# Quadrant moves of transposed attention probabilities: 16 SBUF-to-SBUF DMAs per block against one DMA to DRAM and four back

## The chip, the cores and the metric

The kernel runs on one core of a Trainium2 chip. The metric is the device time in microseconds (us) of one execution; three runs of the kernel before were timed, and one execution was recorded by the hardware profiler. Inside the core, TensorE (PE) multiplies matrices, VectorE (DVE), ScalarE (ACT) and GpSimd (POOL) do the elementwise work, and SyncE (SP) issues nearly all DMAs. Each engine works through its own instructions in order; semaphores hold an instruction back until what it reads is there.

## The reference

Two layers over a batch of 128 blocks of 128 x 512 fp32 numbers. Layer 0 mixes rows with `adj`, layer 1 is an attention with 8 heads of 64 over the 128 rows of each block, masked by `adj`.

```python
# layer 0: both weights are adj, so C - A is the bias b alone
A = einsum('od,bdn->bon', adj, x)
x1 = layernorm(x + max_n(relu(A + b)))       # the maximum is over the 512 columns
# layer 1
q, k, v = split(x1 @ w_qkv)                  # 8 heads of 64
p = softmax(where(adj == 0, -inf, q k^T / 8))
o = (p v) @ w_proj + b_proj
z = o + layernorm(o) * ln_gamma + ln_beta
out = layernorm(x1 + z)
```

## The kernel before

One block is one batch element: its 128 rows lie on the 128 SBUF partitions. Four blocks make a group (`G` = 4). The loop over steps `s` runs every stage once per step, for different blocks: in step `s` the scores of block `s`, the attention product and the projection of block `s-1`, the inner tail of block `s-2`, the output of block `s-3`, the layer 0 of block `s+11` and its normalization and transpose one step later, as block `s+10`; and two of the eight q/k products of the next group and one v product. So a step holds one block's share of every stage, and the blocks in flight are spread over about fourteen steps. At the end of the batch the q/k/v work stops first (no next group), then layer 0 has long stopped, and the last steps hold attention and tails alone.

What sets the order. The order of the matmuls is written out by hand: `pin` (`keep_in_program_order`) makes TensorE issue them as the program has them, which is, per step: scores (L214), a q/k unit (L174), layer 0 (L135), a q/k unit, the attention product of the block before (`attend`, L267), a v unit (L190), the projection (`project`, L284). The order on the other engines and on SP's DMA queue is chosen by the framework's scheduler when the kernel is built, from the dependences and the program order. Tiles come from pools with a given number of buffers (`bufs`, 2 if nothing else is said); whoever writes into a buffer again waits for its last reader.

Two transposes need help from DMA. VectorE's stream transpose works within 32 x 32 squares, so after it each square is transposed, but still in the quadrant of 32 partitions where it was. `move_quadrants` (L121 to L125) then moves 4 x 4 pieces between quadrants, with one DMA each, all issued by SP. It is used at two places:

- `prob_transpose` (L251 to L260), once per block. `softmax_div` has divided the exponentials, VectorE transposes the 128 x 1024 probabilities into `pu` (L255), and 16 DMAs of 32 partitions x 1 KB each bring them to `pT`. `attend` (L262 to L275) of the next step multiplies by `pT` on TensorE (L267, 16 small matmuls), and ACT copies the result to `oT` for the projection. `pu` and `pT` have two buffers each.
- `layer0_transpose` (L152 to L164), for every fourth block: the four blocks of a group are transposed into one tile `xt`, and after the fourth one 16 DMAs of 64 KB bring them to `x1T`, which the q/k and v products of the next group read three steps later.

SP's queue holds besides these the load of one `x` block per step (L79, from HBM) and the store of one result `res` per step (L310, to HBM).

Of the kernel before, what the change touches and what calls it, by code (L numbers as in the profile page):

```python
# [9 lines left out]
F32 = mybir.dt.float32  # L10
# [6 lines left out]
def kernel(  # L17
# [22 lines left out]

    nc = tc.nc
    B, P, D = x.shape
    H = 8
# [5 lines left out]
    Q = 4  # L51
    QS = P // Q
# [4 lines left out]
    const = ctx.enter_context(tc.tile_pool(name="const", bufs=1))  # L57
    sb = ctx.enter_context(tc.tile_pool(name="sb", bufs=2))
    small = ctx.enter_context(tc.tile_pool(name="small", bufs=4))
    ps_s = ctx.enter_context(tc.tile_pool(name="ps_s", bufs=3, space=bass.MemoryType.PSUM))  # L60
    ps_m = ctx.enter_context(tc.tile_pool(name="ps_m", bufs=4, space=bass.MemoryType.PSUM))
    ps_o = ctx.enter_context(tc.tile_pool(name="ps_o", bufs=1, space=bass.MemoryType.PSUM))
# [58 lines left out]
    def move_quadrants(dst, src):  # L121

        for i in range(Q):
            for q in range(Q):
                nc.sync.dma_start(out=dst[i][ds(q * QS, QS)], in_=src[q][ds(i * QS, QS)])  # L125
# [125 lines left out]
    def prob_transpose(b):  # L251

        p = prob.pop(b)
        u = sb.tile([P, Q, H, QS], F32, tag="pu", name=f"pu_{b}")
        nc.vector.transpose(  # L255
            u.rearrange("p q h b -> p h q b"), p.rearrange("p h (q a) -> p h q a", q=Q)
        )
        t = sb.tile([P, Q, H, QS], F32, tag="pT", name=f"pT_{b}")
        move_quadrants([t[:, i] for i in range(Q)], [u[:, q] for q in range(Q)])
        pT[b] = t  # L260

    def attend(b):  # L262
# [53 lines left out]
    for s in range(-(LA + 1), B + 4):  # L316
        g, j = divmod(s, G)
        nxt = g + 1
        has_next = 0 <= nxt < B // G
        if s > -(LA + 1):  # L320
            on(load, s + LA + 3)
        on(scores, s)
        on(tail_outer, s - 3)
        on(layer0_norm, s + LA)
        on(layer0_transpose, s + LA)
        if has_next:
            qk_unit(nxt, 2 * j)
        on(layer0, s + LA + 1)
        if has_next:
            qk_unit(nxt, 2 * j + 1)  # L330
        on(tail_inner, s - 2)
        on(attend, s - 1)
        if has_next:
            v_unit(s + G)
        on(layer0_stats, s + LA + 1)
        on(project, s - 1)
        on(softmax_div, s)
        on(prob_transpose, s)
        on(tail_residual, s - 2)
# [41 lines left out]
```

## Time and profile before

| | |
|---|---|
| device time, median of 3 runs | 2524.27 us (2522.86 to 2524.66) |
| profiled execution: its own time / its span | 2525.88 us / 2524.1 us |
| TensorE's granted clock, mean over the span | 0.948 |
| VectorE busy | 1532.6 us (61%), 2690 instructions |
| ScalarE busy | 700.1 us (28%) |
| GpSimd busy | 787.9 us (31%) |
| DMA | 407480 packets, 174.80 MB; queue of SP 27.6% of 16 engines |
| HBM read / written | 38.60 MB / 33.55 MB |
| longest wait: ACT for VectorE's row maximum (L236 for L233) | 1093.2 us in 128 times |

The device time of the profiled execution is its span, from the first to the last instruction, and 1.8 us around it. An engine's share of busy time says how much of the span it has work in hand; a wait of an engine matters only where that engine, or what waits for it in turn, sets the end. ACT's 1093.2 us is such a harmless wait: ACT has 28% of work and waits because it has nothing else to do.

### The profile page before, as it was taken

To read this page: it belongs to the slowest core of one execution; us is meant where nothing else is said; L and a number is where in the kernel's file an instruction comes from. 1 tells how busy PE (TensorE), PEld (TensorE's weight loads), DVE (VectorE), ACT (ScalarE), POOL (GpSimd) and SP (SyncE) were. 2 spreads that over 40 slices of the span, in tenths; PEclk is the share of its full clock that TensorE was granted. 3 is DMA by queue.
4 is the path that set the end of the run, shared out by engine and by line. 5 is a ranking of instruction groups with operands and counts; after the bars stand their busy time and mean duration, and the time that the engine had idled before them with its cause. 6 is when DMAs were issued, how large, how long until landed. Compare 5 with 4: busy or idle time off the path is not lost. (4 is left out here: it accounts for less than half of the span.)

```text
span 2524.1 us, 28394 instructions
## 1 busy us (share of the span) xinstructions
PE 2278.5 (90%) x8449; PEld 1087.7 (43%) x8449; DVE 1532.6 (61%) x2690; ACT 700.1 (28%) x2561; POOL 787.9 (31%) x1159
## 2 busy tenths in 40 slices
PE   5999999999999999999999999999999999998974
PEld 2444444444444444444444444444444444444432
DVE  4465666656666656656656666666656666655554
ACT  1222223232223232222232232322232322232221
POOL 1123333332333333333333333333333323332323
PEclk8999999999999999999999999999999999999986
DMA  5222332322332322332222233322332322322111
GB/s 165 48 62 68 71 76 66 72 68 68 71 77 65 72 68 69 71 74 67 71 67 70 71 75 69 71 69 68 71 72 68 72 70 66 70 62 60 41 47 42
DMA packets 407480, 174.80 MB, mean 69 GB/s; under 512 B 307488, under 2 KB 373152, under 8 KB 407328
## 3 DMA queue, kind: packets, MB, share of 16 engines
q1 hardware_dynamic: 405792, 168.02, 27.6%
q10 hardware_dynamic: 1536, 4.98, 0.5%
q8 instruction: 68, 1.11, 0.2%
q14 instruction: 84, 0.69, 0.1%
HBM read 38.60 MB, written 33.55 MB: 29 GB/s over the span
## 5 line engine op out<-in xcount | busy, mean ns | idle before, releaser
L174 PE MATMUL pq<-x1T,wqkv 128*128 128x512 f32 x2048 | 934.0, 600 | 16.3 <-DMA x1T<-xt 16.3
L236 ACT ACTIVATE s<-s,nmax 128x128 f32<-128x128 f32 x1024 | 396.1, 388 | 1093.2 <-DVE nmax L233 1093.2
L174 PEld LDWEIGHTS pq<-x1T,wqkv 128*128 128x128 f32 x2048 | 380.3, 190 | 462.9 <-issue 447.9
L190 PE MATMUL pv<-wqkv,x1T 128*128 128x512 f32 x1024 | 509.5, 643 | 0.0
L284 PE MATMUL pp<-wproj,oT 128*128 128x512 f32 x1024 | 473.5, 607 | 3.6 <-ACT oT L275 3.6
L267 PE MATMUL po<-pT,v 128*64 128x128 f32 x2048 | 168.7, 315 | 197.6 <-DMA pT<-pu 188.9
L304 DVE TENSOR_TENSOR z<-z,x 128x512 f32<-128x512 f32 x128 | 88.6, 692 | 420.5 <-POOL z L299 420.5
L284 PEld LDWEIGHTS pp<-wproj,oT 128*128 128x128 f32 x1024 | 199.4, 195 | 255.4 <-issue 249.7
L190 PEld LDWEIGHTS pv<-wqkv,x1T 128*128 128x128 f32 x1024 | 199.9, 206 | 232.7 <-issue 229.5
L114 POOL TENSOR_SCALAR rs_o<-mv_o 128x1 f32<-128x1 f32 x128 | 28.4, 222 | 769.8 <-DVE mv_o L112 769.8
L288 DVE TENSOR_TENSOR o<-pp,bp_bc 128x512 f32<-128x512 f32 x128 | 88.5, 692 | 295.8 <-PE pp L284 295.8
L267 PEld LDWEIGHTS po<-pT,v 128*64 128x64 f32 x2048 | 134.5, 158 | 295.2 <-issue 270.1
L297 POOL TENSOR_TENSOR z<-z,ga_bc 128x512 f32<-128x512 f32 x128 | 162.2, 1267 | 281.1 <-DVE z L119 281.1
L114 POOL TENSOR_SCALAR rs_y<-mv_y 128x1 f32<-128x1 f32 x128 | 28.3, 221 | 627.3 <-DVE mv_y L112 623.3
L198 ACT COPY v<-pv 128x512 f32<-128x512 f32 x128 | 74.9, 585 | 428.4 <-PE pv L190 428.4
L236 ACT ACTIVATION_READ_ACCUMULATOR s<-s,nmax 128x1 f32 x1024 | 191.4, 187 | 0.0
L223 DVE SCALAR_TENSOR_TENSOR s<-pss,mask 128x512 f32<-128x512 f32 x256 | 168.2, 658 | 2.9 <-PE pss L214 2.9
L214 PEld LDWEIGHTS pss<-qkT 64*128 64x128 f32 x2048 | 124.3, 188 | 97.2 <-issue 97.2
L299 POOL TENSOR_TENSOR z<-z,o 128x512 f32<-128x512 f32 x128 | 162.7, 1271 | 10.0
L298 POOL TENSOR_TENSOR z<-z,be_bc 128x512 f32<-128x512 f32 x128 | 162.3, 1268 | 10.0
L249 DVE TENSOR_TENSOR s<-s,rec 128x1024 f32<-128x1024 f32 x128 | 156.8, 1225 | 4.4
L255 DVE STREAM_TRANSPOSE pu<-s 128x1024 f32<-128x1024 f32 x128 | 157.1, 1227 | 0.1
(37 smaller groups left out, 1829.3 us busy)
## 6 DMA issues: line engine op xcount, KB each, us to landing
pT<-pu SPq DMA_DIRECT2D x2048, 32.0 KB, 1.8
x<-in_x_dram SPq DMA_DIRECT2D x128, 256.0 KB, 2.8
x1T<-xt SPq DMA_DIRECT2D x512, 64.0 KB, 2.3
out_dram<-res SPq DMA_DIRECT2D x128, 256.0 KB, 2.2
wqkv<-in_L_gnn_w_qkv_dram ACTq DMA_DIRECT2D x4, 768.0 KB, 7.5
wproj<-in_L_gnn_w_proj_dram ACTq DMA_DIRECT2D x1, 1024.0 KB, 9.2
bp_bc<-in_L_gnn_b_proj_dram ACTq DMA_DIRECT2D x1, 256.0 KB, 8.0
ga_bc<-in_L_gnn_ln_gamma_dram ACTq DMA_DIRECT2D x1, 256.0 KB, 8.3
```

The source lines that it names most:

```text
L174: pin(nc.tensor.matmul(pq, lhsT=wqkv[:, c, ts(m, P)], rhs=x1T[g][:, c, :], start=(c == 0), stop=(c == KC - 1),))
L190: pin(nc.tensor.matmul(pv, lhsT=x1T[g][:, c, ts(j, P)], rhs=wqkv[:, c, ds(2 * D, D)], start=(c == 0), stop=(c == KC - 1),))
L214: pin(nc.tensor.matmul(pss[par][:, pr, :], lhsT=qkT[g][rows, pr, ts(j, P)], rhs=qkT[g][rows, KC + pr, ts(j, P)], start=True, stop=True,))
L223: nc.vector.scalar_tensor_tensor(s[:, par], pss[par], SCALE, mask.unsqueeze(1).to_broadcast([P, NP, P]), ALU.mult, ALU.add,)
L236: nc.scalar.activation(p[:, i, :], p[:, i, :], AF.Exp, bias=nmax[:, i : i + 1], accum_out=sums[:, i : i + 1],)
L249: nc.vector.tensor_tensor(p, p, rec.unsqueeze(2).to_broadcast([P, H, P]), ALU.mult)
L255: nc.vector.transpose(u.rearrange("p q h b -> p h q b"), p.rearrange("p h (q a) -> p h q a", q=Q))
L267: pin(nc.tensor.matmul(po[ds(par * HD, HD), pr, :], lhsT=v[:, ds((2 * pr + par) * HD, HD)], rhs=t[:, :, par * NP + pr, :], start=True, sto ...
L284: pin(nc.tensor.matmul(pp, lhsT=o[:, c, :], rhs=wproj[:, c, :], start=(c == 0), stop=(c == KC - 1)))
L297: nc.gpsimd.tensor_tensor(z, z, ga_bc, ALU.mult)
L298: nc.gpsimd.tensor_tensor(z, z, be_bc, ALU.add)
L299: nc.gpsimd.tensor_tensor(z, z, o, ALU.add)
```

## The change

The helper stays as it is for `layer0_transpose`. `prob_transpose` no longer calls it. It takes a scratch tile `hop` in DRAM (three buffers), writes the whole of `pu` there with one DMA (128 partitions x 4 KB, 512 KB), and then reads it back with four DMAs, one for each quadrant of `pT`: each fills 32 partitions with four pieces of 1 KB per partition (128 KB). All five are issued by SP. The numbers in `pT` and their place are those of before. The reads take what the write has put into `hop`, so they depend on it.

```diff
@@ pools
     small = ctx.enter_context(tc.tile_pool(name="small", bufs=4))
+    dram = ctx.enter_context(tc.tile_pool(name="dram", bufs=3, space=bass.MemoryType.DRAM))
@@ prob_transpose
         nc.vector.transpose(
             u.rearrange("p q h b -> p h q b"), p.rearrange("p h (q a) -> p h q a", q=Q)
         )
+        hop = dram.tile([Q, QS, Q, H * QS], F32, tag="hop", name=f"hop_{b}")
+        nc.sync.dma_start(
+            out=hop.rearrange("i a q f -> (i a) (q f)"), in_=u.rearrange("p q h b -> p (q h b)")
+        )
         t = sb.tile([P, Q, H, QS], F32, tag="pT", name=f"pT_{b}")
-        move_quadrants([t[:, i] for i in range(Q)], [u[:, q] for q in range(Q)])
+        for q in range(Q):
+            nc.sync.dma_start(
+                out=t[ds(q * QS, QS)].rearrange("a i h b -> a i (h b)"),
+                in_=hop[:, :, q].rearrange("i a f -> a i f"),
+            )
         pT[b] = t
```

## The prediction

> **What bounds the kernel now.** I read the page's busy shares first, then the table of waits, then the timelines of TensorE and of SP around one stall, then the landing times of the DMAs.
>
> ```profile
> PE 2278.5 (90%) x8449; PEld 1087.7 (43%) x8449; DVE 1532.6 (61%) x2690; ACT 700.1 (28%) x2561; POOL 787.9 (31%) x1159
> ...
> PE po L267 <- DMA pT<-pu: 188.9, 43, 8.6
> PE pq L174 <- DMA x1T<-xt: 16.3, 1, 16.3
> ```
>
> TensorE has work for 90% of the span, and nearly all that it waits for is one thing: in 43 of 128 blocks the attention product waits for `pT`, 188.9 us in all. TensorE's timeline over five steps shows where (start, duration, line, operation; in brackets the idle time before and its releaser):
>
> ```profile
> 1247.15 1.09 PE L267 MATMUL po<-pT,v 128*64 128x128 f32 x16
> 1248.18 3.70 PE L190 MATMUL pv<-wqkv,x1T 128*128 128x512 f32 x8
> ...
> 1260.73 3.60 PE L174 MATMUL pq<-x1T,wqkv 128*128 128x512 f32 x8
> 1269.60 1.98 PE L267 MATMUL po<-pT,v 128*64 128x128 f32 x16 [5.27 <-DMA pT<-pu]
> 1271.50 4.42 PE L190 MATMUL pv<-wqkv,x1T 128*128 128x512 f32 x8
> ...
> 1288.30 1.09 PE L267 MATMUL po<-pT,v 128*64 128x128 f32 x16
> ...
> 1305.47 1.09 PE L267 MATMUL po<-pT,v 128*64 128x128 f32 x16
> ```
>
> One `attend` to the next is 17.1 us where nothing stalls (1230.05 to 1247.15), then 22.45, 18.70, 17.17 us. The stall of 5.27 us comes once per four steps, and it costs more than itself: after it the 16 matmuls take 1.98 instead of 1.09 us, and the v unit 4.42 instead of 3.70; TensorE runs at half clock for a moment. SP's timeline of the same stretch shows the cause:
>
> ```profile
> 1235.64 10.02 SPq L125 DMA_DIRECT2D pT<-pu  x16
> 1245.75 0.63 SPq L125 DMA_DIRECT2D x1T<-xt  x1
> 1246.48 0.56 SPq L310 DMA_DIRECT2D out_dram<-res  x1
> 1247.10 10.67 SPq L125 DMA_DIRECT2D x1T<-xt  x15
> 1257.89 10.26 SPq L125 DMA_DIRECT2D pT<-pu  x16
> ```
>
> Sixteen issues of `pT` keep SP busy for 10.0 us. In every fourth step sixteen issues of `x1T` (0.63 + 10.67 us) stand in front of the next `pT`: its `pu` is ready at 1252.80 (VectorE's transpose starts at 1251.57 and takes 1.23), but SP gets to it at 1257.89. The last piece lands at about 1269.5, and TensorE could have started at 1264.3. So the bound is TensorE, plus one stall per group that SP's issuing makes. Without `x1T` ahead it just fits: `pu` ready 1235.61, `attend` 1247.15.
>
> ```profile
> pT<-pu SPq DMA_DIRECT2D x2048, 32.0 KB, 1.8
> x<-in_x_dram SPq DMA_DIRECT2D x128, 256.0 KB, 2.8
> x1T<-xt SPq DMA_DIRECT2D x512, 64.0 KB, 2.3
> out_dram<-res SPq DMA_DIRECT2D x128, 256.0 KB, 2.2
> ```
>
> The last number is the median from issue to landing. It hardly grows with size: eight times the bytes of a `pT` piece add 0.4 us to HBM and 1.0 us from HBM.
>
> **What the Trainium skill says.** "Perfetto Trace Analysis", section What "DMA-bound" means: a kernel can be bound on the issuing engine's sequencer, whose track is then solid DMA slices, and fewer, larger transfers help. The trace agrees: 1235.64 to 1268.15 on SP is one row of issues. "DMA: Bandwidth & Descriptors", section Anatomy of one DMA: about 2 us of every DMA is fixed, most of it the confirmation that the last byte landed, and HBM is the heaviest target. The medians of 1.8 to 2.8 us agree in size; a store to HBM (2.2) is no worse than an `x1T` piece inside SBUF (2.3). Same page, section Two DMAs through the same engine are not ordered: a DMA that reads what another wrote must be issued only after the first one's semaphore, so the reads wait on SP for the write to land; no run so far shows such a wait. "TensorE: Matmul & The Clock Gate", section What's actually happening: after an idle window of about 3.4 us the array falls to half clock and needs about as long to recover. The trace agrees: gaps up to 1.14 us are followed by 1.09 us for the 16 matmuls, the gap of 5.27 us by 1.98.
>
> **The change part by part.** I call T the time from the end of the transpose into `pu` until the last part of `pT` has landed, SP being free. Now it is 0.1 us to the first issue, fifteen issue intervals of 10.02/16 = 0.63 (9.4), and 1.8 for the last to land: 11.3 us.
>
> *Removed:* sixteen issues per block, 10.0 us of SP, and their sixteen landings.
>
> *Added, the write.* Its issue costs 0.33 to 0.56 us (what L310's stores take). Landing: the store of 256 KB takes 2.2; twice the bytes are eight more packets of 2 KB per DMA engine, at 84 ns each (median of the packet records), 0.7: 2.9 us. Bounds: 2.2 (no more than half the bytes) and 4.1 (the slowest store, 3.4, plus 0.7).
>
> *Added, the wait.* SP stands still for these 2.9 us. Behind it on SP are the four reads, the next `x` load (two steps ahead of its use), `x1T` (three steps ahead) and the store (nobody waits for it but its buffer), so only the reads matter.
>
> *Added, four reads.* Issue 0.63 each as now (0.71 at most, the interval of `x1T`, which has more and smaller pieces): 1.9 from first to last. Landing: the 256 KB load takes 2.8, these have 128 KB in pieces of 1 KB, a little less: 2.6. Bounds: 1.8 (a `pT` piece today) and 4.3 (the slowest landing of any L125 DMA).
>
> T = 0.1 + 2.9 + 0.1 + 1.9 + 2.6 = 7.6 us; from the bounds, 6.1 to 10.7 (last with 2.1 for the issues). SP is held for about 5.5 us per block instead of 10.0, wait included. Buffers do not tighten: `pu` is free when the write has landed, earlier than now, `hop` has three, and the read into `pT` needs an `attend` one step earlier to be over, as now. The bytes through the DMA engines rise by 128 x 512 KB, 67 MB to 174.8; their share of 27.6% leaves room.
>
> *Moved: the collision.* With SP free at about 1241 instead of 1245.66, `x1T` starts earlier; its first issue may even fall into the wait (`xt` is ready at 1237.96). If the store stays between the first and the second issue, it waits for `res` (1242.74) and is done at 1243.3; fifteen issues of 0.71 end at 1254.0; the write follows, and `pT` is there at 1254.0 + 7.5 = 1261.5. TensorE wants it at 1264.25. The stall is gone with 2.7 us to spare. Without `x1T`, `pT` is there 7.6 us after `pu`, 3.9 us before TensorE asks. Next in line is then TensorE itself, at 17.1 us per step.
>
> *The sum*, against the profiled execution. From the first `attend` (109.6) to the 117th (2305.6) are 116 steps in 2196.0 us; 116 x 17.12 (17.10, and a little for the 17.17 to 17.2 that some smooth steps show) = 1986: 210 us less. The next six steps, to 2415.34, take 109.7; their TensorE work is 16.25 us each (2365.25 to 2381.49), 97.5: 12 less. In the last five steps TensorE waits for the loop attend, projection, scores, softmax, transpose, T, attend, which carries two steps: 33.94 us now (2433.20 to 2467.14), and it shrinks by 11.7 - 7.6 = 4.1; 2.5 times: 10 less. The start, up to the first `attend`, and the 23 us after the last one stay. 2525.88 - 232 = 2294 for this execution, and as the median of the runs lies 1.6 lower, 2292.
>
> **The rivals.**
>
> *A, slower hop, smaller gain.* From `attend` of one block to the `pu` two blocks later is 1252.8 - 1230.05 = 22.7 us, so two steps cannot be shorter than 22.7 + T. That is 34.2, TensorE's own pace, at T = 11.5, and the collided step is late from T = 10.2 on. A gap below some 3.4 us costs itself, a larger one 1.6 more. With T = 12.5, the collided step is 2.3 late and all others lose 0.5: 29 x 2.3 + 116 x 0.5 = 125 us back, about 2417. For it: a write and a read of the same scratch in HBM within microseconds is in no row of the trace. Against: no store or load of HBM in the steady part is near what it needs.
>
> *B, the hop eats all.* A step costs 2196/116 = 18.93 us now, so the break-even is 2 x 18.93 - 22.7 = 15.2 us for T. If write and read both landed like the 768 KB weights at the start (7.5 us), T = 17.1, two steps 39.8, a step 19.9: +112 over the 116 steps, some +25 behind them, 2660. Against: those weights were loaded all at once, together with the first blocks.
>
> *C, the reads are queued behind `x1T`; slower.* The scheduler sees that the reads are not ready when the write is issued, and may place SP's other work between. If all sixteen `x1T` issues and the store stand there, the reads start at 1254.0, `pT` lands at 1258.6, and `attend`, wanted at 1247.15, is 11.4 late plus 1.6 for the clock: 13.0 per group against the present 75.7 - 68.4 = 7.3. 29 groups x 5.7 = 165 slower, less the 22 won at the end: some 2670. It decides from seven such issues on (3.9 us of slack hold five or six at 0.71), and costs more than now from about twelve. For it: the store already stands between `x1T` issues today. Against: the reads belong to the earlier step and would be ready some 1 us after `xt` is.
>
> That the change moves different data is excluded by its indices; that TensorE stands at a lower clock when it no longer pauses is possible, but a stretch of 85 us (55 to 140) is on record at full clock.
>
> **How the numbers follow.** Forecast 0.63, within 2275 to 2320 (T anywhere from 6.1 to 10.7). A 0.18, reaching from 2320 to 2490. B 0.08, of which 0.04 ends near no change. C 0.11. Faster: 0.63 + 0.18 = 0.81. Within 0.2% (5 us, about what a measurement of this kernel can tell from no change): 0.04. Slower: 0.04 + 0.11 = 0.15. B and C are left out of the range, 0.19; it reaches from 2275 to 2450, over most of A.
>
> **What would show it.** Right: no wait of L267 for `pT` in the steady part, steps of 17.1 us throughout, the clock at full between 140 and 2250, SP waiting some 3 us per block for the write, T near 7.6 us. The write's landing shows the first term, the reads' the last. Wrong: stalls at every step (A or B), or SP's timeline with `x1T` between the write and the reads (C).

## The result, and the profile after

The changed kernel takes 2697.49 us (median; 2695.24 to 2698.57) against 2524.47 us for the kernel before on the same chip: a ratio of 1.0684, 95% interval 1.0665 to 1.0702. It is slower by 173 us, where 232 us less were forecast, and outside the stated range. The span of the profiled execution is 2696.2 us against 2524.1.

The lines of the page and of the table of waits that answer to those shown of the kernel before (the change moves the line numbers; `attend` is now L277):

```profile
PE 2265.9 (84%) x8449; PEld 1081.7 (40%) x8449; DVE 1532.5 (57%) x2690; ACT 699.6 (26%) x2561; POOL 789.7 (29%) x1159
...
PE po L277 <- DMA pT<-hop: 374.4, 35, 12.2
```

TensorE's and VectorE's busy times hardly changed. The wait for `pT` has become rarer, 35 times instead of 43, and twice as long in sum, 374.4 us instead of 188.9: the time went exactly where the prediction hoped to take it from. TensorE's timeline over five steps (start, duration, line, operation, idle time before):

```profile
1241.03 1.09 PE L277 MATMUL po<-pT,v 128*64 128x128 f32 x16
...
1258.13 1.09 PE L277 MATMUL po<-pT,v 128*64 128x128 f32 x16
...
1286.59 1.98 PE L277 MATMUL po<-pT,v 128*64 128x128 f32 x16 [11.28 <-DMA pT<-hop]
```

A step takes 17.10 us where nothing is late, and the next one 28.46. The pattern is once per group as before, but the stall is 11.28 us instead of 5.27. SP's timeline over the same steps:

```profile
1229.62 0.33 SPq L261 DMA_DIRECT2D hop<-pu  x1
1232.24 1.75 SPq L266 DMA_DIRECT2D pT<-hop  x4
...
1246.72 0.32 SPq L261 DMA_DIRECT2D hop<-pu  x1
1249.07 1.27 SPq L127 DMA_DIRECT2D x1T<-xt  x2
1250.44 1.99 SPq L266 DMA_DIRECT2D pT<-hop  x4
1253.74 0.36 SPq L320 DMA_DIRECT2D out_dram<-res  x1
1254.14 9.36 SPq L127 DMA_DIRECT2D x1T<-xt  x14
1263.82 0.34 SPq L261 DMA_DIRECT2D hop<-pu  x1
1270.85 0.34 SPq L320 DMA_DIRECT2D out_dram<-res  x1
1280.91 0.32 SPq L261 DMA_DIRECT2D hop<-pu  x1
1281.34 4.31 SPq L266 DMA_DIRECT2D pT<-hop  x8
```

The first write is followed by its four reads, as the diff has them. The write at 1263.82, the one behind `x1T`, is not. Behind it stand a store, then the write of the *next* block, and only then the reads of both blocks, eight of them. The next write waits for the next `pu`, whose transpose ends at 1280.9 (VectorE starts it at 1279.66 and takes 1.23). So the data of this block lie in DRAM from about 1266.4 on, nobody fetches them for 15 us, and TensorE stands.

The hop itself is fast. The page's landing times:

```profile
hop<-pu SPq DMA_DIRECT2D x128, 512.0 KB, 2.6
pT<-hop SPq DMA_DIRECT2D x512, 128.0 KB, 3.4
```

In the step at 1229.62 the last read is issued at 1233.6 and lands some 3.2 us later, about 7.2 us after `pu` was ready. The forecast for this T was 7.6.

The balance, from the starts of `attend` in the profiled execution: the 116 steps that took 2196.0 us now take 2376.6 (+181), the six after them 112.0 instead of 109.7 (+2), the last five 76.0 instead of 85.6 (-10). A group of four steps is 28.9 + 18.8 + 17.1 + 17.1 = 81.9 us, against 75.7 before and 68.4 without any stall; 30 steps of the whole execution are of the long kind.

### The profile page after: what moved, and what is told of

Read it like the earlier page. It is cut to its first block, busy times and chain, and to the rows that moved or that the text cites. A ratio compares the mean times of both kernels' runs of the same rounds, so it can differ in the third digit from the quotient of the medians.

```text
span 2696.2 us, 26511 instructions
## 1 busy us (share of the span) xinstructions
PE 2265.9 (84%) x8449; PEld 1081.7 (40%) x8449; DVE 1532.5 (57%) x2690; ACT 699.6 (26%) x2561; POOL 789.7 (29%) x1159
## 4 chain that ended last, share of the span: by engine, by line
PE 73%; DVE 10%; POOL 7%; DMA 5%; SPq 3%; issue 2%; ACT 0%; POOLq 0%; ACTq 0%
PE pq L176 26%; PE pv L192 18%; PE pp L294 17%; PE po L277 6%; DMA pT<-hop 4%; PE pss L216 4%; PE pa L137 3%; SPq L266 2%; POOL z L308 2%; POOL z L307 2%; POOL z L309 2%; DVE nmax L235 1%; DVE pu L257 1%; DVE o L298 1%; DVE st_o L112 1%
## 5 line engine op out<-in xcount | busy, mean ns | idle before, releaser
L192 PE MATMUL pv<-wqkv,x1T 128*128 128x512 f32 x1024 | 500.1, 633 | 0.0
L277 PE MATMUL po<-pT,v 128*64 128x128 f32 x2048 | 168.8, 316 | 374.4 <-DMA pT<-hop 374.4
L277 PEld LDWEIGHTS po<-pT,v 128*64 128x64 f32 x2048 | 133.7, 159 | 470.4 <-issue 470.4
L285 ACT COPY oT<-po 128x512 f32<-128x512 f32 x128 | 74.9, 585 | 409.2 <-PE po L277 400.0
```

The source lines that it names most:

```text
L192: pin(nc.tensor.matmul(pv, lhsT=x1T[g][:, c, ts(j, P)], rhs=wqkv[:, c, ds(2 * D, D)], start=(c == 0), stop=(c == KC - 1),))
L277: pin(nc.tensor.matmul(po[ds(par * HD, HD), pr, :], lhsT=v[:, ds((2 * pr + par) * HD, HD)], rhs=t[:, :, par * NP + pr, :], start=True, sto ...
```

## The experiments

Three theories were put against each other. O: the loss is the place of the reads on SP's queue, and nothing else. H: a hop through HBM is too slow for the steps with `x1T`. S: the sixteen `x1T` issues clog SP, whatever comes behind them.

### Reads held directly behind their own write

Only edges of issue order on SP's queue are added, no wait for completion. They keep whatever SP is given later (loads, `x1T`, writes into `hop`, stores, each wrapped as the load is here) behind the last read, so that all 128 writes are followed at once by their four reads:

```diff
+    last_read = []
+    def behind_reads():
+        return tc.issue_after(last_read[0].ins) if last_read else nullcontext()
...
-        nc.sync.dma_start(out=t, in_=x[f])
+        with behind_reads():
+            nc.sync.dma_start(out=t, in_=x[f])
...
         for q in range(Q):
-            nc.sync.dma_start(
+            rd = nc.sync.dma_start(
...
+        last_read[:] = [rd]
```

> Theory O (order): the change loses time only because, once per group, the four reads of a block stand on SP's queue behind the write of the next block, so that they wait for the next block's transpose. With the reads held directly behind their own write, T is 7.5 us in every step, the wait of L267 for pT goes from 374 us to under 30, steps are 17.1 us throughout, and the time is what the prediction gave for its likeliest case, 2292 us (2275 to 2320). Rival H (the hop itself is slow): reads through DRAM land too late in the steps with x1T whatever the order, so the time stays above 2600. Rival S (SP is clogged by the sixteen x1T issues, which still stand ahead of one write per group): a stall of 2 to 5 us per group is left, 2370 to 2480.

Measured: 2290.5 us (2290.37 to 2291.66), ratio to the kernel before 0.906 (0.9044 to 0.9075). TensorE is busy for 97% of the span. TensorE's and SP's timelines around an `x1T` step:

```profile
1205.02 1.09 PE L286 MATMUL po<-pT,v 128*64 128x128 f32 x16
...
1222.12 1.09 PE L286 MATMUL po<-pT,v 128*64 128x128 f32 x16
```

```profile
1201.07 11.60 SPq L133 DMA_DIRECT2D x1T<-xt  x16
1212.77 0.56 SPq L269 DMA_DIRECT2D hop<-pu  x1
1215.69 1.75 SPq L274 DMA_DIRECT2D pT<-hop  x4
```

Same DMAs, same bytes, 407 us less than the changed kernel. Every step of the steady part is 17.10 or 17.11 us. In the `x1T` step `pu` is ready at 1210.68, the write gets its turn at 1212.77, the last read lands near 1220.5, and TensorE asks for it at 1222.12. SP stands still for the write 128 times, 299.2 us in all, and in the steady part TensorE never waits for `pT`; only the last five blocks do, 23.1 us in all. H and S fall: neither the hop nor the sixteen issues ahead of it cost anything here. Theory O's forecast of 2292 us is met.

### Reads held before the next write only

A smaller dose of the cause: the reads may not stand behind the next block's write, all else is left to the scheduler.

```diff
+        with tc.issue_after(last_read[0].ins) if last_read else nullcontext():
             nc.sync.dma_start(
                 out=hop.rearrange("i a q f -> (i a) (q f)"), ...
```

> The reads of a block are held before the write of the next block, and nothing else is fixed; once per group the scheduler now puts one store and two loads of x between the write and its reads. Theory O: the second load waits for the buffer that ScalarE's layer 0 of the next step frees, so the reads go out some 12 us late instead of 17, attend is 6 us late plus 1.6 for the clock: 30 groups x 8 = 240 over 2292, about 2530 (2450 to 2600), between e1b and the changed kernel. Rival H: above 2600, as before. Rival S: as e1b, since x1T stands where it stood.

Measured: 2552.94 us (2551.73 to 2559.22), ratio 1.0103 (1.0084 to 1.0122). SP's timeline where it happens, and TensorE's line of that step:

```profile
1203.66 0.34 SPq L263 DMA_DIRECT2D hop<-pu  x1
1210.68 0.34 SPq L323 DMA_DIRECT2D out_dram<-res  x1
1211.13 5.39 SPq L81 DMA_DIRECT2D x<-in_x_dram  x2
1216.61 1.81 SPq L268 DMA_DIRECT2D pT<-hop  x4
1220.74 0.34 SPq L263 DMA_DIRECT2D hop<-pu  x1
```

```profile
1221.74 1.98 PE L280 MATMUL po<-pT,v 128*64 128x128 f32 x16 [6.60 <-DMA pT<-hop]
```

The store waits 7 us for `res`, the second load 5 us for its buffer, and the four reads behind them go out 13 us after the write instead of 17.5. The stall is 6.60 us instead of 11.28, and (2552.9 - 2290.5)/30 = 8.7 us per group, where 8 were expected: the cost follows the place.

### Reads late in every step

The full dose: for blocks 4 to 123 an edge of issue order puts the reads of a block behind the write of the next.

```diff
+        for rd in held:
+            tc.add_manual_dep(
+                rd.ins, wr.ins.name,
...
+            )
+        held.clear()
```

> The changed kernel with the misplacing made the rule: for blocks 4 to 123 the reads of a block are held behind the write of the next one. Theory O: attend of a block starts 22.7 us (attend to the next pu) + some 5.5 us (issue of write and reads, landing 3.4) after attend of the block before, plus 1.6 for the clock: 29.6 us per step instead of 17.1 for 120 blocks, 2290 + 120 x 12.5 = 3790 (3600 to 3900), L267 waiting about 11 us in nearly every block. If the order is not what costs, it stays near 2700.

Measured: 3944 us, one execution. L287 (the attention product there) waits 1446.2 us for `pT` in 124 blocks, 11.7 us each:

```profile
1216.41 1.98 PE L287 MATMUL po<-pT,v 128*64 128x128 f32 x16 [11.53 <-DMA pT<-hop]
...
1246.80 1.98 PE L287 MATMUL po<-pT,v 128*64 128x128 f32 x16 [11.28 <-DMA pT<-hop]
...
1278.18 1.97 PE L287 MATMUL po<-pT,v 128*64 128x128 f32 x16 [12.11 <-DMA pT<-hop]
```

The time is above the range that was given. The two steps shown are 30.39 and 31.38 us instead of 29.6: the stalls are 11.3 and 12.1 us where 10.9 were reckoned (29.6 - 17.1 - 1.6), and what is left of the steps, 19.1 and 19.3 us, is 2.0 to 2.2 us above 17.1, where 1.6 were set for the slow clock. The mechanism is the expected one, its price above 17.1 us 6% to 14% higher than reckoned (13.3 and 14.3 us against 12.5). Over the whole run it is (3944 - 2290.5)/120 = 13.8 us per step.

### `x1T` on another queue, with the hop and without it

What makes the scheduler misplace the reads, and what made the old stall? Two pairs of kernels give `move_quadrants` of `x1T` to another engine's queue:

```diff
-            move_quadrants([t[:, :, :, i] for i in range(Q)], [u[:, q] for q in range(Q)])
+            move_quadrants([t[:, :, :, i] for i in range(Q)], [u[:, q] for q in range(Q)], nc.scalar)
```

(or `nc.gpsimd` as the last argument; the helper issues from the engine that it is given).

> The changed kernel with the sixteen x1T DMAs per group issued by ScalarE. SP's order is then write, reads in every step without being told. Theory O: the stall goes although nothing was done to the hop, 2292 to 2330 (ScalarE gets 10 us of issues per group, which may delay an exponential by some us). Rival H: above 2600. Rival S: 2292 to 2330 too; e1b tells O and S apart.

> The kernel before, sixteen pT DMAs per block inside SBUF, with x1T issued by ScalarE. If its stall is the collision on SP that the prediction read from the trace, it goes: 2300 to 2340, as pT lands 11.3 us after pu with 11.5 allowed, so that small waits are left. If the sixteen issues of pT are too slow by themselves, it stays near 2524.

> The changed kernel with x1T's DMAs issued by GpSimd instead of ScalarE. SP's order is then write, reads in every step. Theory O: no wait of L267 for pT. GpSimd has 31% work, but it computes the row factors that normalize waits for; if one of its issues takes some 1 us, VectorE is held up to 16 us once per group, part of which reaches TensorE: 2300 to 2550. If T were at fault, L267 would go on waiting.

> The kernel before with x1T's DMAs issued by GpSimd. The collision on SP is gone, so L267's wait for pT falls from 189 us to under 60; what GpSimd's issues hold up is as in the run beside it: 2320 to 2570.

| `x1T` issued by | with the hop | 16 DMAs, as before |
|---|---|---|
| SP | 2697.5 us | 2524.5 us |
| ScalarE | 2599.62 us, ratio 1.0283 (1.0268 to 1.0299) | 2760.17 us, ratio 1.0918 (1.0901 to 1.0934) |
| GpSimd | 2290.89 us, ratio 0.9072 (0.9051 to 0.9093) | 2365.45 us, ratio 0.9367 (0.9345 to 0.9389) |

ScalarE was a miss: both expectations were some 270 to 460 us too low. The 5 to 12 us waits for `pT` in the steady part are gone there, and another stands in their place, once per group. From the changed kernel with `x1T` on ScalarE, TensorE's line, then ScalarE's timeline just before it, then two pieces of the chain of waits that ends in TensorE's line, the second released by the first:

```profile
1222.90 5.30 PE L294 MATMUL pp<-wproj,oT 128*128 128x512 f32 x8 [8.11 <-ACT oT L285]
```

```profile
1210.46 10.66 ACTq L127 DMA_DIRECT2D x1T<-xt  x6
...
1222.28 0.58 ACT L285 COPY oT<-po 128x512 f32<-128x512 f32 x1
```

```profile
1215.15 2.62 DMA hop<-pu
...
1217.80 3.39 DMA x1T<-xt
```

The copy of the attention product, which the projection waits for, stands behind `x1T`'s issues in ScalarE's own order. "10 us of issues may delay an exponential by some us" was the error: what stands behind the issues matters, not how busy the engine is. Nor do the issues follow each other: there is none between 1212.5 and 1217.8. In the trace the issue at 1217.80 waits for the same semaphore that reports the landing of SP's write into `hop`; that write is issued at 1215.15, when its `pu` is ready, and lands at 1217.78. So the two queues are tied together by semaphores that their DMAs share. In the kernel without the hop ScalarE's next copy stands still behind the issues for 374.8 us in 28 times, and the table of waits puts that down to the landing of `pT` pieces that SP issues.

GpSimd has no such instruction: what it computes is needed by VectorE only, and with the hop TensorE is busy for 97% of the span in spite of the issues; the time is 9 us below the range that was expected. With the hop, SP's order is write, reads in every step without any edge, and the time is that of the first experiment. So the misplacing of the reads is tied to `x1T`'s sixteen issues on the same queue; why the scheduler answers to them in this way was not examined. Without the hop, taking `x1T` off SP removes the 5 us stalls of the kernel before: its wait for `pT` falls to 89.1 us, where under 60 was expected. Of the rest 37 us fall to the last five blocks, and most of the other pieces are 0.7 to 0.8 us, in every other step.

### The kernel before with a better order on SP

How much of the gain needs the hop at all? Here the sixteen `pT` DMAs stay, and `x1T` follows behind `pT` in two halves in successive steps, by the same kind of edge:

```diff
+                later.extend([(dst, src, (0, 1)), (dst, src, (2, 3))])
...
+        with behind_last():
+            last[:] = [move_quadrants([t[:, i] for i in range(Q)], [u[:, q] for q in range(Q)])]
+        if later:
+            with behind_last():
+                last[:] = [move_quadrants(*later.pop(0))]
```

> The kernel before, with the order on SP set by hand and no hop: pT's sixteen DMAs go first, and x1T's sixteen follow behind pT in two halves of eight, in two successive steps. If the old stall was a matter of who stands first on SP, it goes: T is still 11.3 us, 11.5 are allowed, so waits of some tenths of a us may be left; the 22 us that the shorter T gives at the end stay away: 2292 + 22 = 2314 (2300 to 2350). If sixteen issues per block are too many for SP in themselves, the stall only moves: above 2450.

Measured: 2385.75 us (2383.57 to 2387.35), ratio 0.9445 (0.9427 to 0.9463): between the two expectations, 72 us above the first. TensorE's timeline, and ScalarE's just before the second of its waits, show what is left:

```profile
1215.33 1.09 PE L282 MATMUL po<-pT,v 128*64 128x128 f32 x16 [0.86 <-DMA pT<-pu]
...
1238.92 3.70 PE L299 MATMUL pp<-wproj,oT 128*128 128x512 f32 x8 [1.77 <-ACT oT L290]
```

```profile
1237.68 0.72 ACT L148 ACTIVATE y<-x,r 128x512 f32<-128x512 f32 x1 [4.79 <-issue]
1238.31 0.57 ACT L290 COPY oT<-po 128x512 f32<-128x512 f32 x1
```

No large stall is left in the steady part, but two small ones are. Sixteen issues of 0.63 us leave a T of 11.3 us where 11.5 are allowed, and every issue in front of them makes it late: TensorE's waits before the attention product add up to some 22 us from block 4 to 116. The larger one is no matter of `pT`. Once per group ScalarE's copy to `oT` stands behind its layer 0 (L148), which waits for a value `r` that VectorE computes late; TensorE's projection then waits, 39 us in 28 times. The order on other engines has changed with the edit too. Of the 236 us between the kernel before and the best one, this reordering brings 139. The 95 from here to the best (2385.75 to 2290.5) are not the hop's alone, since the wait for `oT` is among them; the pair with `x1T` on GpSimd, whose programs differ in the hop alone, puts the hop at 75.

## Why the prediction was wrong

- *The bound* was read rightly: TensorE at 17.1 us per step, and one stall per group from the collision of `pT` and `x1T` on SP. The kernel before with `x1T` on GpSimd and the one with the better order on SP remove that stall and win 159 and 139 us.
- *The write and the reads* were sized rightly in the sum, with errors that offset each other. The write lands in 2.6 us (forecast 2.9), the reads in 3.0 to 3.4 (forecast 2.6), their issue interval is 0.43 us (forecast 0.63); T is 7.2 (forecast 7.6). The fixed 2 us that the prediction quotes from the Trainium skill ("DMA: Bandwidth & Descriptors", section Anatomy of one DMA) are given there for DMAs that GpSimd issues; here SP issues them, and the measured landings decide.
- *The wait* is where it failed. The prediction listed what stands behind the waiting SP, the four reads, a load, `x1T`, a store, and concluded that "only the reads matter"; and in the collided step it let "the write follows, and `pT` is there at 1254.0 + 7.5". Both take it for granted that the reads come next on the queue. The order on SP is not written in the kernel; it is the scheduler's. Once per group it put a store and the next block's write between, and both wait for work of the next step. The runs show this step in place of the assumed one: with the reads where the prediction had them, the time is 2290.5 us, against 2292 forecast.
- *The sum* was right for the kernel that it describes. With the reads directly behind their write a step takes 17.10 us against 17.12, and the last five steps 75.1 us, where 10 off 85.6 were forecast.
- *Rival C* named the mechanism, the reads queued behind other work of SP, and its price of 2670 is 27 us from what came. That the price fits is luck, because its place was wrong: it put sixteen `x1T` issues between, and what stood there was the next block's write. Two `x1T` issues do stand between the write at 1246.72 and its reads, and TensorE does not wait for them. It got a chance of 0.11, on the argument that the reads "would be ready some 1 us after `xt` is"; in the run they were ready at about 1266.4 and still went out behind the next write, at 1281.34. Rivals A and B, a slow hop, did not occur.
- *The clock*: a stall of 11 us is again followed by 1.98 us for the sixteen matmuls instead of 1.09, as a stall of 5 us was. With no stalls TensorE holds the full clock through the whole steady part of the first experiment: its granted clock is 1.00 from 110 to 2077 us. The 85 us at full clock that the prediction calls on record lie from about 44 to 130 us on the time axis of the views, not from 55 to 140; the window from 55 to 140 has a mean of 0.96.

## What to carry to other kernels

A DMA that must wait for another DMA splits one queue entry into two with a gap between, and whoever fills the gap may wait for something far later. Where a framework orders the queue, pin the dependent DMA behind its producer, or look at the built order before trusting a sum of durations. A queue that also computes, like ScalarE's here, is a good place for extra DMAs only if nothing that the bound engine needs stands behind them, and if the DMAs do not wait there for semaphores that another queue's DMAs hold.

## What the runs showed of the hardware that was not expected

A round trip of 512 KB through HBM took 7.2 us from `pu` to `pT`, less than the 11.3 us of sixteen copies inside SBUF: the write lands in 2.6 us and each read in 3.0 to 3.4, where the sixteen copies of 32 KB land in 1.8 us each and need 10.0 us to be issued. The interval of issues on SP differs by form: 0.63 us for the copies of 32 partitions x 1 KB inside SBUF, 0.43 for the reads of 128 KB from HBM. `x1T`'s DMAs land in 4.4 us when GpSimd issues them beside the hop, and in 2.3 when SP does; ten issues in a row on GpSimd took 0.67 us each, fourteen on SP also 0.67, sixteen on SP in the first experiment 0.72.
